# A selective-scan block on one core: pairs of states added by accumulating DMAs instead of by GpSimd

## The chip, the cores and the metric

The kernel runs on one core of a Trainium2 chip. A core has five engines that each work through their own queue in order: TensorE (PE, with its weight loads as PEld), VectorE (DVE), ScalarE (ACT), GpSimd (POOL) and SyncE (SP, which here only issues DMAs). Sixteen DMA engines move data. The metric is the device time of one execution in microseconds. Three runs of the kernel before gave 1902.2 us (median), 1901.79 us (lowest) and 1904.03 us (highest).

## The reference

The input x is (128, 64, 256): 128 sequences of 64 steps and 256 channels, all in float32. Two blocks follow each other, both steered by one condition vector of 512 numbers per sequence.

The first is a linear attention with 16 heads: layer norm, three projections, a softmax of q over the 16 channels of a head and of k over the 64 steps (masked), two small products for each head, a layer norm scaled and shifted by the condition, a projection, and x added back.

The second is a Mamba layer. After a modulated layer norm and a permutation of the steps it computes, cut to what matters here:

```python
xm, z = split(h @ W_in, 2)                 # 512 channels each
xm = silu(conv4(xm) + conv_b)
dtr, Bm, Cm = split(xm @ W_xp, [64, 80])   # 64, 16 and 16 columns
dt = softplus(dtr @ W_dt + b_dt)
A = -exp(A_log)                            # 512 channels x 16 states
# for every step t:
hst = hst * exp(dt_t * A) + (dt_t * x_t) * B_t     # 512 x 16 states
y_t = sum over the 16 states of hst * C_t
y = (y + xm * D_param) * silu(z)
out = x + gate * unpermute(y @ W_out)
```

The recurrence has 128 x 512 x 16 independent states of 64 steps each. They are multiplied by C and added up over the 16 states of a channel. The change touches that sum.

## The kernel before

**Groups.** The 128 sequences are worked in 16 groups of 8 (`NG`, `NB`). For each group, `prepare` computes everything up to dt, w = dt * x, B and C. `scan` does the recurrence, once for each half of the group (4 sequences), and `finish` does the output projection, the gate and the store.

**The scan.** In one half, the loop `m` runs over four blocks of 128 channels and the loop `x` over the two 64-channel halves of a block. One pair (m, x) has one tile `hs` of 128 partitions x (2 x 2 x 8 x 64): partition = 64 channels x 2 halves of the states, then `ii` (two pairs of sequences), sequence in the pair, 8 states (`SJ`), 64 steps. A tile holds 2048 numbers per partition, 1 MB in all. For each `ii`:

- TensorE multiplies `uT` by `diag` and so writes the input term into `hb`, two banks of PSUM (two such buffers);
- ScalarE has made `decay`, the exponentials, 8 instructions for each tile;
- VectorE runs one `tensor_tensor_scan` of 128 x 1024;
- the product with C (`ct`) is made either by VectorE, out of PSUM, or by GpSimd ("apart"), in place in `hs`. The set `APART` gives GpSimd 12 of the 16 products of a half, so 24 of the 32 of a group.

When both `ii` are done and (half, m) is in `PAIRED` (all but half 1, m = 3), GpSimd adds the upper four of the eight states of the tile to the lower four, 128 x 1024 again. TensorE then adds what is left, and the two halves of the states, into `yacc`: with `fold` as weights it runs over j = 0..3 (over 8 states where no pairs were added) for both x. VectorE multiplies `yacc` by silu(z).

There are four `hs` buffers (`NHS`), three `decay` buffers, three `dt2` and four `ct` buffers, two `hb` and one `yacc`.

**Order.** Nothing is left to a scheduler at run time. The class `Plan` records every call as a node; units such as the eight matmuls of one `hb` are one node. The table `ORDER` gives each node of each part (`scan0`, `prepare` and so on) a place, `PERIOD` (100000) being one group, and `order()` lists the nodes by place, holding back those whose inputs or buffers are not there yet. Each engine's queue is that list cut to its own instructions, so `prepare` of later groups is interleaved with the scans. All recorded instructions carry the line of `emit()` in the profile (L486), so groups of instructions are told apart by the names of their tiles.

All loads and stores are issued by SP: `dt2` and `ct` of the scans come back out of HBM (`dt_d`, `c_d`) with each partition half or broadcast that the scan needs.

Of the kernel before, what the change touches and what calls it, by code (L numbers as in the profile page):

```python
# [12 lines left out]
ALU = mybir.AluOpType  # L13
# [4 lines left out]
B, T, D, E = 128, 64, 256, 512  # L18
# [7 lines left out]
NG = B // NB  # L26
KD = D // P
KE = E // P
KI = DI // P
HD = P // 2  # L30
NC = DI // HD
SJ = DS // 2
# [4 lines left out]
APART = {(m, x, 1 - x) for m in range(KI) for x in range(2)} | {(m, 0, 0) for m in range(4)}  # L37
PAIRED = {(h, m) for h in range(2) for m in range(KI)} - {(1, 3)}
# [13 lines left out]
        -995092, -990106, -990248, -972121, -595796, -212864, -174753, -196191, -212939,  # L52
        -961099, -963028, -647496, -239082, -809048, -585679, -903380, -392982, -995853,
        -998690, -998658, -978564, -998761, -1000000, -972303, -1000000, -971839, -998153,
        -992335, -995851, -808931, -992190, -997171, -819048, -989678, -634347, -998162,
        -993953, -989802, -449288, -1000000, -1000000, -789091, -987936, -370078, -825915,
        -678524, -613218, -698586, -662425, -968759, -606956, -473579, -999671, -999858,
        -990255, -998888, -1000000, -1000000, -994652, -999181, -1000000, -985837, -960273,
        -998934, -999181, -977310, -993627, -944637, -971780, -811427, -664040, -784771,
        -664039, -677889, -888439, -689643, -663391, -840908, -663146, -663413, -727553,  # L60
        -663328, -789092, -832193, -851274, -740157, -1000000, -964818, -974366, -731822,
        -991350, -862414, -944797, -1000000, -921394, -812212, -380935, -379583, -183624,
        -176975,
    ],
    "first0": [
        -1000000, -978376, -630660, -998627, -997704, -1000000, -1000000, -1000000, -997299,
        -996885, -999569, -990645, -1000000, -996822, -999447, -994659, -989968, -998495,
        -987832, -959171, -958623, -976292, -981641, -975857, -960993, -985546, -959733,
        -995015, -963408, -949376, -970868, -999959, -953582, -955776, -993088, -953651,
        -944012, -970225, -1000000, -944938, -979597, -934713, -951862, -947285, -943580,  # L70
        -940278, -995331, -833149, -933011, -946878, -857180, -908964, -902556, -965635,
        -819890, -819889, -819891, -737922, -740147, -744759, -714085, -731823, -763169,
        -872482, -767462, -755421, -755080, -770282, -776097, -653828, -571415, -712761,
        -732409, -727706, -749172, -755428, -731824, -729395, -672745, -471240, -405022,
        -408492, -488949, -405021, -370547, -645082, 46765, -640238, -723310, -763006, -782420,
        -754953, -774218, -760167, -340878, -371799, -759582, -766127, -751948, -776216,
        -776050, -776898, -754988, -340856, -341375, -290888, -210442, -361958, -210446,
        -188783, -211959, -188951, -177248, -213375, -188950, -192852, -204116, -196189,
        -187951, -211128, -204115, -208765, -208765, -188958, -178898, -163476, -180505,
        -158338, -165498, -145454, -155745, -145454, -172674, -146435, -126094, -127959,  # L80
        -172671, -145457, -155746, -133032, -154259, -138626, -127958, -133490, -232875,
        -133033, -144477, -156111, -773778, -126843, -123327, -132724, -119680, -1000000,
        -118311, -118822, -133033, -140386, -895462, -117437, -118344, -133405, -95145, -991619,
        -92484, -93161,
    ],
    "first2": [
        -989917, -914702, -325416, -961231, -898579, -969532, -956870, -935784, -960145,
        -999952, -793395, -785227, -1000000, -993454, -946566, -953153, -948506, -938449,
        -939387, -758886, -792923, -687377, -766280, -667266, -630921, -638864, -565697,
        -769280, -446058, -462407, -440447, -811646, -624057, -561269, -488663, -432081,  # L90
        -435680, -401509, -796577, -486505, -426280, -431834, -395880, -434914, -490816,
        -399758, -353104, -240433, -380946, -417054, -360040, -431462, -367222, -397314,
        -358066, -357955, -211127, -358065, -351132, -343370, -274423, -208764, -335285,
        -346455, -775180, -772723, -765469, -764949, -778615, -198584, -203309, -774446,
        -782667, -983648, -984891, -982282, -984450, -980988, -165217, -178508, -123412,
        -147465, -178443, -145453, -155852, -127265, -57778, -132562, -158314, -978503, -988197,
        -978277, -997227, -998661, -119700, -118821, -993949, -980523, -117713, -113567,
        -126885, -114336, -117349, -107072, -107049, -104840, -101480, -116857, -101599, -90423,
        -89609, -86117, -79331, -79567, -121935, -96516, -95027, -94510, -94006, -93342, -92924,
        -105967, -92054, -85660, -137236, -96517, -95039, -94637, -94094, -57435, -73060,  # L100
        -51702, -90005, -50756, -49688, -69739, -69740, -88328, -48446, -45829, -630507, -26868,
        -18979, -46514, -53088, -42764, -50412, -205762, -989257, 6466, -35323, -44427, -216090,
        -984626, 8399, -25010, -42762, -95308, -984980, 8489, 16549, -42761, -74750, -672321,
        9524, -14450,
    ],
    "scan0_first": [
        -128446, -162321, -151313, -139747, -132474, -182139, -144153, -163187, -122764,
        -120446, -122763, -122741, -122775, -122619, -122759, -122742, -133003, -112983,
        -156884, -165753, -108962, -112179, -115646, -119159, -119978, -113196, -116946,
        -111650, -116947, -107108, -111854, -255984, -109585, -110801, -163615, -117229,  # L110
        -103941, -105375, -101837, -96833, -111020, -92232, -277702, -233357, -106504, -111651,
        -107071, -106505, -107097, -104186, -107048, -104879, -252777, -123872, -108466,
        -122522, -99858, -192554, -441320, -101598, -98871, -96846, -106013, -98873, -101829,
        -102382, -101479, -153484, -99862, -186581, -105117, -107253, -93200, -116016, -80008,
        -80006, -53963, -35228, -99131, -109970, -91775, -80007, -93795, -93376, -101175,
        -88674, -96847, -96832, -89984, -46602, -134677, -62212, -44885, -43484, -190998,
        -96509, -94571, -93795, -88329, -96510, -96769, -94573, -94572, -40567, -39885, -30010,
        -94992, -45773, -140866, -20555, -85810, -1094, 10253, -38273, -131760, -128140, -93313,
        -90382, -93377, -93269, -74516, -88328, -88673, -89608, -39386, -74983, -42626, -43686,
        -81144, -27441, 9922, -25352, -27196, -39947, -27596, -39184, -22373, -26684, -30454,  # L120
        8401, 9790, -1426, -36436, -19644, 10273, -4455, 11186, -34099, 19364, -24524,
    ],
    "finish0_first": [
        135714, 27333, 126520, 135825, 160280, 161813, 21135, 495636,
    ],
    "scan1_first": [
        -411767, -317259, -15340, -452280, -353099, -25361, -473315, -347887, -48840, -89188,
        -13745, -59991, -27083, -29839, 6232, -59649, 10975, -75102, 19200, 11087, -821,
        -297741, -291099, 1780, -13121, -25608, -18694, 7747, -13412, 131, -12218, 10789, 4646,
        -309099, 11434, -160608, -105030, -152161, 24753, 8163, 33100, -44420, -264583, -215312,  # L130
        13333, 11181, 12647, 13277, -35685, 11118, -12268, 13544, 21792, -121531, -114359,
        18780, -101067, -155325, -57931, -21737, -5479, 14694, 26131, 11762, -22060, -24964,
        14539, 23071, -106218, 33427, 32746, -80584, -142524, 22028, 43491, -129616, 49509,
        -18791, -272321, -261752, 15526, 3471, 31319, -25503, 20208, 30558, 27720, 29985, 42577,
        -35042, -143989, 36726, -30002, -135919, -582334, 40363, 40602, 30962, 37930, 39676,
        43084, 47815, 32963, 50445, 59070, 48398, 41875, 61090, 36526, -377950, 54088, 65664,
        73884, 105441, -235375, -166644, 43077, 44885, 13734, 44774, 45454, 48182, 47616, 40078,
# [1171 lines left out]
```

## Time and profile before

| what | before |
|---|---|
| three runs, median (lowest to highest) | 1902.2 us (1901.79 to 1904.03) |
| the profiled execution: span from its first to its last instruction | 1900.2 us |
| busy, share of the span: PE | 1768.6 us, 93% |
| DVE | 1770.5 us, 93% |
| ACT | 1703.3 us, 90% |
| POOL | 1769.5 us, 93% |
| DMA: share of the 16 engines on SP's queue | 25.6% |
| products on POOL (hs <- hs,ct) | 384 of 2367 ns |
| pair additions on POOL (hs <- hs) | 224 of 2363 ns |
| products on DVE (hs <- hb,ct) | 128 of 1223 ns |
| scans on DVE | 512 of 2273 to 2275 ns |

The median of the three runs is 2.0 us above the span of the profiled execution. "Busy" is the time in which at least one instruction of the engine runs; instructions that only issue a DMA, wait or load a register are not counted. "Idle before" a group is the time for which the engine stood still just ahead of its instructions, and the releaser is what ended that wait. A wait line reads: engine and tile that waited, whom it waited for, microseconds in all, how many times, the longest.

### The profile page before, as it was taken

Reading aid. Unit: us, or ns where it says so; the run is one execution under the profiler, and the core shown is the slowest. Engines: PE = TensorE matmul, PEld = TensorE weight load, DVE = VectorE, ACT = ScalarE, POOL = GpSimd, SP = SyncE. Lnnn points to the kernel's source line nnn. Section 1 sums busy time; section 2 is a strip of 40 time slices with the busy share of each in tenths; the row PEclk is TensorE's granted clock in tenths of the full one; section 3 lists DMA queues with packets and bytes.
Section 4 is the critical chain, followed back from the end, with each engine's and each line's share of the span. In section 5 each row is a group of like instructions: output and inputs, shape, how many; then the busy total and the mean of one; then the engine's idle time right before and its main releaser. Section 6 shows DMA issues by size and latency. Waiting matters only on the chain.

```text
span 1900.2 us, 32360 instructions
## 1 busy us (share of the span) xinstructions
PE 1768.6 (93%) x11304; PEld 927.5 (49%) x11304; DVE 1770.5 (93%) x1625; ACT 1703.3 (90%) x3996; POOL 1769.5 (93%) x1440
## 2 busy tenths in 40 slices
PE   7788999999999999999999999999999999999776
PEld 5454544545454454545545454554545445454333
DVE  6579899999999999999999999999999999999886
ACT  5889999998999999899999989999899999989762
POOL 3579899999999999999999999999999999999996
PEclk9899999999999999999999999999999999999998
DMA  5311322204132230323213132220413222041320
GB/s 148 80 51 40 79 82 71 79 21 126 42 88 74 63 95 26 109 61 87 74 43 98 37 101 68 82 79 26 115 38 87 82 74 78 20 119 37 102 63 12
DMA packets 173291, 135.71 MB, mean 71 GB/s; under 512 B 30820, under 2 KB 157272, under 8 KB 173128
## 3 DMA queue, kind: packets, MB, share of 16 engines
q1 hardware_dynamic: 173128, 133.64, 25.6%
q8 instruction: 90, 1.47, 0.3%
q14 instruction: 73, 0.60, 0.1%
HBM read 98.84 MB, written 34.75 MB: 70 GB/s over the span
## 4 chain that ended last, share of the span: by engine, by line
POOL 38%; ACT 28%; PE 10%; DVE 8%; issue 6%; DMA 3%; SPq 0%; POOLq 0%; DVEq 0%; ACTq 0%
POOL hs L486 28%; ACT decay L486 13%; DVE hs L486 4%; POOL diag L486 3%; ACT h L486 3%; POOL w L486 3%; DVE xz L486 3%; PE hb L486 2%; ACT kT L486 2%; ACT L482 2%; DVE hb L486 2%; ACT xz L486 2%; PE zp L486 2%; PE kp L486 1%; ACT xn L486 1%
## 5 line engine op out<-in xcount | busy, mean ns | idle before, releaser
L486 ACT ACTIVATE decay<-dt,nA 128x252 f32<-128x252 f32 x2048 | 865.9, 501 | 60.7 <-DMA dt<-dt_d 38.9
L486 POOL TENSOR_TENSOR hs<-hs,ct 128x1024 f32<-128x1024 f32 x384 | 900.7, 2367 | 14.8 <-DVE hs L486 14.7
L486 DVE TENSOR_TENSOR_SCAN hs<-decay,hb 128x1024 f32<-128x1024 f32 x384 | 863.0, 2273 | 38.6 <-PE hb L486 24.6
L486 PE MATMUL hb<-diag,uT 64*64 64x512 f32 x4096 | 532.2, 614 | 68.0 <-DVE hs L486 67.1
L486 POOL TENSOR_TENSOR hs<-hs 128x1024 f32<-128x1024 f32 x224 | 525.8, 2363 | 6.1 <-DVE hs L486 1.1
L486 PE MATMUL yacc<-hs,fold 128*64 128x256 f32 x2304 | 284.6, 392 | 17.2 <-ACT yacc L486 13.9
L486 DVE TENSOR_TENSOR_SCAN hb<-decay,hb 128x1024 f32<-128x1024 f32 x128 | 291.1, 2275 | 4.6 <-PE hb L486 4.6
L486 PEld LDWEIGHTS hb<-diag,uT 64*64 64x64 f32 x4096 | 120.6, 132 | 332.1 <-DVE hs L486 148.3
L486 PEld LDWEIGHTS yacc<-hs,fold 128*64 128x64 f32 x2304 | 163.8, 139 | 147.3 <-POOL hs L486 56.2
L482 ACT ACT_TABLE_LOAD x158 | 202.7, 1283 | 3.4 <-PEq L1297 0.8
L486 DVE TENSOR_TENSOR hs<-hb,ct 128x1024 f32<-128x1024 f32 x128 | 156.5, 1223 | 7.9 <-PE yacc L486 3.2
L486 DVE SCALAR_TENSOR_TENSOR xz<-xp,vec,xz 128x504 f32<-128x504 f32 (+5 forms) x204 | 140.2, 698 | 9.5 <-ACT xz L486 5.2
L486 POOL TENSOR_TENSOR diag<-fold,bT 128x1024 f32<-128x1024 f32 x64 | 121.3, 1909 | 12.9 <-ACT bT L486 12.9
L486 PE MATMUL zp<-h,win 128*128 128x512 f32 (+1 forms) x272 | 120.1, 575 | 1.1 <-DVE xz L486 1.1
L486 PE MATMUL xp<-h,win 128*128 128x512 f32 (+1 forms) x272 | 119.2, 580 | 0.7 <-DVE xz L486 0.6
L486 PE MATMUL yop<-wout,xz 128*128 128x256 f32 x512 | 117.5, 383 | 0.0
L486 PEld LDWEIGHTS yop<-wout,xz 128*128 128x128 f32 x512 | 94.7, 190 | 25.2 <-ACT decay L486 10.6
L486 POOL TENSOR_TENSOR w<-dt,xz 128x512 f32<-128x512 f32 (+1 forms) x68 | 82.0, 1217 | 14.3 <-ACT dt L486 11.2
L486 ACT ACTIVATE yacc<-xz,vec 128x256 f32<-128x256 f32 x128 | 61.0, 477 | 33.1 <-PE yacc L486 33.0
L486 ACT ACTIVATE h<-gtp,mods 128x64 f32<-128x64 f32 x256 | 78.8, 418 | 3.9 <-PE gtp L486 3.9
L486 PEld LDWEIGHTS zp<-h,win 128*128 128x128 f32 x272 | 49.7, 190 | 65.9 <-issue 62.6
L486 PEld LDWEIGHTS xp<-h,win 128*128 128x128 f32 x272 | 48.7, 189 | 67.3 <-issue 47.6
(145 smaller groups left out, 2358.7 us busy)
## 6 DMA issues: line engine op xcount, KB each, us to landing
ct<-c_d SPq DMA_DIRECT2D x128, 256.0 KB
dt<-dt_d SPq DMA_DIRECT2D x256, 128.0 KB
dt_d<-dt SPq DMA_DIRECT2D x60, 256.0 KB
ga<-gate_d SPq DMA_DIRECT2D x64, 128.0 KB
xr<-x_d SPq DMA_DIRECT2D x32, 256.0 KB
out<-xr SPq DMA_DIRECT2D x32, 256.0 KB
xt<-in_x SPq DMA_DIRECT2D x15, 512.0 KB
x_d<-xt SPq DMA_DIRECT2D x15, 512.0 KB
```

The lines of the kernel that those rows point to most:

```text
L482: engine.preload_act_table_set(loaded)
L486: getattr(engine, method)(*real, **kreal)
```

## The change

The pair addition is no longer an instruction on GpSimd's vector path. GpSimd issues a DMA that reads the upper four states of the tile and adds them to the lower four in SBUF. In each tile it moves 128 partitions x 4 runs of 256 numbers, 512 runs of 1 KB. It is issued for the same (half, m) as before, so 224 times. The products are divided anew: VectorE keeps 5 of the 32 of a group (`ON_VECTOR`), GpSimd makes 27. The last group has sets of its own, which hold the same members. The table `ORDER` is replaced throughout. Buffers, matmuls, scans, exponentials and SP's DMAs are the same in number and shape.

```diff
-APART = {(m, x, 1 - x) for m in range(KI) for x in range(2)} | {(m, 0, 0) for m in range(4)}
-PAIRED = {(h, m) for h in range(2) for m in range(KI)} - {(1, 3)}
+ALONE = {(1, 3)}
+ON_VECTOR = {(0, 0, 1, 1), (0, 2, 1, 1), (1, 0, 1, 1), (1, 1, 1, 1), (1, 3, 1, 1)}
+ALONE_LAST = {(1, 3)}
+ON_VECTOR_LAST = {(0, 0, 1, 1), (0, 2, 1, 1), (1, 0, 1, 1), (1, 1, 1, 1), (1, 3, 1, 1)}
...
 ORDER = {
     "setup": [
...
     def scan(g, half):
+        alone, on_vector = (
+            (ALONE_LAST, ON_VECTOR_LAST) if g == NG - 1 else (ALONE, ON_VECTOR)
+        )
...
-                    apart = (m, x, ii) in APART
+                    apart = (half, m, x, ii) not in on_vector
...
                 ready = pl.writers(hs[:, 0])
-                if (half, m) in PAIRED:
-                    pl.gpsimd.tensor_tensor(
-                        hs[:, :, :, : SJ // 2, :].rearrange("p i b j t -> p (i b) (j t)"),
-                        hs[:, :, :, : SJ // 2, :].rearrange("p i b j t -> p (i b) (j t)"),
-                        hs[:, :, :, SJ // 2 :, :].rearrange("p i b j t -> p (i b) (j t)"),
-                        op=ALU.add,
-                    )
+                if (half, m) not in alone:
+                    pairs = hs.rearrange("p i b j t -> p (i b) (j t)")
+                    near, far = pairs[:, :, : SJ // 2 * T], pairs[:, :, SJ // 2 * T :]
+                    pl.gpsimd.dma_start(out=near, in_=far, accum_op=ALU.add)
...
-            last = SJ // 2 if (half, m) in PAIRED else SJ
+            last = SJ if (half, m) in alone else SJ // 2
```

The numbers of `ORDER` are left out here. Where the text speaks of the new order, it means the list that they give on each engine.

## The prediction

> **What bounds the kernel now.** I read first the table of windows, because a share over the whole span mixes stages. Columns: window, its length, then the busy us of PE, PEld, DVE, ACT and POOL (number of instructions), the granted clock, the DMA share and GB/s.
>
> ```profile
> 200.00:1700.00 1500.00, 1443.07 (x9378) 756.54 (x9375) 1456.94 (x1299) 1414.00 (x3317) 1460.84 (x1145) 1.00 0.27 73
> 1700.00:1800.00 100.00, 86.16 (x534) 38.83 (x530) 91.31 (x68) 88.73 (x197) 97.50 (x61) 0.98 0.25 74
> 1800.00:1900.00 100.00, 73.34 (x456) 35.21 (x450) 77.53 (x51) 43.65 (x108) 83.04 (x37) 0.89 0.13 39
> ```
>
> From 200 to 1700 us four engines are all but full: POOL 97.4%, DVE 97.1%, PE 96.2%, ACT 94.3%. Only in the last 200 us does one stand out: POOL, with 180.5 us of work against 168.8 on DVE. Second, the groups by line and shape (busy us, mean ns of one | idle before):
>
> ```profile
> L486 POOL TENSOR_TENSOR hs<-hs,ct 128x1024 f32<-128x1024 f32 x384 | 900.7, 2367 | 14.8 <-DVE hs L486 14.7
> L486 POOL TENSOR_TENSOR hs<-hs 128x1024 f32<-128x1024 f32 x224 | 525.8, 2363 | 6.1 <-DVE hs L486 1.1
> L486 DVE TENSOR_TENSOR hs<-hb,ct 128x1024 f32<-128x1024 f32 x128 | 156.5, 1223 | 7.9 <-PE yacc L486 3.2
> ```
>
> Products and pair additions are 1426.5 us of POOL, 89.2 us for each of 16 groups. The same instructions fill 1174.6 us of the window from 200 to 1700 (windows of the tile hs alone), so it holds 1174.6 / 89.2 = 13.2 groups and one group lasts 113.6 us. In each group POOL works 110.7 us, DVE 110.4, PE 109.3, ACT 107.1. Taking work off POOL alone can therefore win at most 113.6 - 109.3 = 4.3 us of a group: PE is next. Third, the waits:
>
> ```profile
> PEld hb L486 <- DVE hs L486: 148.3, 121, 4.0
> PE hb L486 <- DVE hs L486: 67.1, 83, 3.8
> PEld yacc L486 <- POOL hs L486: 56.2, 53, 3.0
> ACT decay L486 <- DMA dt<-dt_d: 38.9, 34, 4.2
> ```
>
> PE stands still mostly for DVE to free hb, and its weight loads wait 56.2 us for the pair additions: PE reaches yacc while POOL is still adding. Fourth, SP's queue, for what a DMA costs (start, us, instruction):
>
> ```profile
> 985.88 0.34 SPq L486 DMA_DIRECT2D c_d<-xd  x1
> 987.60 1.26 SPq L486 DMA_DIRECT2D ct<-c_d  x2
> 990.71 0.34 SPq L486 DMA_DIRECT2D dt_d<-dt  x1
> 993.45 1.22 SPq L486 DMA_DIRECT2D dt<-dt_d  x2
> L486 SPq DMA_DIRECT2D ct<-c_d x128: 573/592/1464, 67.1 to 1817.6; - x128
> ```
>
> A load that needs a store is issued once the store has landed: 1.72 us after its issue for the 32 KB of c_d, 2.74 us for the 256 KB of dt_d. The last line is min/median/max of an issue: 592 ns for ct, a transfer of 64 x 8 = 512 runs.
>
> **The change, part by part.**
>
> 1. Pair additions leave POOL's vector path: 14 a group x 2.363 = 33.1 us off POOL.
>
> 2. Three more products a group move from DVE to POOL: 3 x 2.367 = 7.1 us onto POOL, 3 x 1.223 = 3.7 us off DVE. DVE falls to 106.7.
>
> 3. In place of each addition POOL issues a DMA of 512 runs. No row shows POOL issuing one, so call its price x. Below it is bounded by SP's 0.59 us for as many runs, above by 2.36 us, POOL's whole pass over the same half tiles; a price over that isn't excluded, because the reads name both source and destination, and a negative one is, because the queue is in order. I take 1.2 us: the row nearest in kind is SP's issue, and POOL needs twice as long as another engine for the same thing in the rows we have (2.367 against 1.223 for a product). POOL then has 110.7 - 33.1 + 7.1 + 14x = 84.7 + 14x = 101.5 us a group. It stays the bound only from x = (110.7 - 84.7) / 14 = 1.86 us. The Trainium skill ("DMA: Bandwidth & Descriptors", Specifications) puts the first byte of GpSimd's path at about 1 us against 0.6 on SP's; as an estimate from that page x would be 1.0 and POOL 98.7 us.
>
> 4. The sum arrives later. The addition took 2.36 us. The two landing times above (stores to HBM, the nearest rows) give 1.72 + (2.74 - 1.72) x 480/224 = 3.9 us for 512 KB, SP's 0.34 us of issue in it. Reading the destination as well as the source can double the moved part (2.3 us more): 3.9 to 6.2, of which I take the middle, 5.0, and with POOL's slower issue (1.2 - 0.34) it is 5.9 us, 3.5 more than the addition. The Trainium skill speaks against this step: "Collectives: The Full Stack", Part 3, says that a reduce by DMA runs at half a copy's rate because it reads two sources; by that page alone I would stand at the upper end, 7.1 us with the issue. No run here shows it yet.
>
> Who waits for that: PE at yacc, with the hb matmuls of later tiles queued behind it, and behind those DVE, which has two hb (4.5 us of scans) in hand. From the last hb matmul of an m to its yacc, PE must be busy for a scan (2.27), a product (2.37 on POOL, 1.22 on DVE) and the sum. Before, that is 7.0 us, or 5.9 where DVE makes the product. The old order has about 6 us of PE work there in the shortest two places (half 0 m = 3, half 1 m = 1) and 10 or more elsewhere, counted with the matmul rows (8 matmuls of hb 1.09 us, 16 of yacc 1.95). The new order has about 7 at (1,1), 11.5 at (1,0), 12 at (0,3), 13 to 20 elsewhere. The new chain is 10.5 us, or 9.4 at (1,1) and (1,0), whose last product is DVE's: PE loses 9.4 - 7.1 = 2.3 us a group at (1,1) and nothing elsewhere.
>
> 5. The four hs buffers. One tile every 7.1 us gives each 28.4 us. It needs 4.5 (scans) + 2.4 + 5.9 + 7.1 (the other x) + 2 (yacc) = 21.9 us, so in the steady part this is covered by 6.5 us. In the last group, without prepare, a tile comes every 5.3 us (85 us of DVE work in 16 tiles): 21.2 us against 20.1. There the cover is gone.
>
> 6. DMA traffic: 224 x 0.5 MB is 117 MB moved once more, 117/134 of the present 25.6% if read once (22 points), 45 points if both are read: 48 to 71% of the 16 engines. They are not full, but dt2 arrives later behind such bursts; ACT's 38.9 us could double. ACT has 6.5 us of slack a group, so I cost 2.4 us more of its waits a group at nothing. Should ACT be the bound, it would cost that much, 34 us.
>
> Everything else keeps its count (158 table loads, all matmuls, all of SP's DMAs), so it costs nothing as long as the new places are no worse; a micro-stall of 1 us a group is in the sum for them.
>
> **Sum.** Steady part: PE 109.3 + 2.3 + 1.0 = 112.6 us a group against 113.6; over 14 groups -14 us. The last 200 us hold 163.6 / 89.2 = 1.83 groups: POOL's 180.5 us fall by 1.83 x (26.0 - 16.8) = 16.8 to 163.7, DVE's to 162. The tight buffers of step 5 and the later sums eat most of that; I take -6 us. Span 1900.2 - 20 = 1880; with the 2.0 us by which the median of the runs stands above it, 1882 us. At its best (PE at the 98.4% that POOL reached in its fullest 100 us, no wait at yacc) a group lasts 111.1: -35, tail -12, 1855. At its worst within this case (ACT's waits partly showing, no gain in the tail) 1898.
>
> **Rivals.**
>
> A. As forecast: POOL is freed, PE becomes the bound. For it: 26 us a group leave POOL's vector path. Against: only 4.3 us can be won. 1855 to 1898. Chance 0.50.
>
> B. The issue is the new bound, on POOL's queue. Nothing in the trace prices it; it decides from x = 1.86. At x = 2.1 POOL has 114.1 us, at its 97.4% 117.1 a group: +3.5 x 14 = +49, 1951. At 2.4, 118.3/0.974 = 121.5: +7.9 x 14 = +110, 2012. Against: SP's 0.59 for as many runs. Just above 1.86 it is 1906. Chance 0.22.
>
> C. The landing is longer than 5 us and PE stands before yacc. It decides from a loss of 3.3 us a group, a chain of 10.4 at (1,1), that is a sum (issue and landing) of 6.9 us. At 9 us the three short places lose 5.4 + 1.0 + 1.6 = 8.0: 109.3 + 8.0 + 1.0 = 118.3, +4.7 x 14 = +66, 1968. For it: both operands are read, and slices of the DMA row stand at 7 to 9 tenths. Against: the new order already leaves 12 us at (0,3), where the old left 6. 1906 to 1968. Chance 0.22.
>
> D. Gain and waits cancel: within 0.2%, 1898.4 to 1906.0. Chance 0.06.
>
> **How the numbers follow.** 0.2% (3.8 us) is about what a measurement of this kernel can tell from no change. Faster 0.50 (A), same 0.06 (D), slower 0.44 (B and C). The forecast is A's, 1882 us, its own range 1855 to 1898. The range for 8 in 10 starts there and reaches through most of B and C to 1985, leaving out B from x = 2.26 on and a little of A below 1855.
>
> **What would show it.** Right: POOL's busy time near 1769.5 - 525.8 + 113.6 = 1357 us with 432 products of 2.37 us; 224 DMAs on POOL's queue whose issue holds it for 1.2 us or so; PE at 97 to 98% between 200 and 1700, its waits before yacc named by a DMA and under 3 us a group; a group of 112.6 us. B: POOL's queue without idle time though its busy share is 71%, DVE and PE waiting for products. C: yacc <- DMA in the waits with well over 100 us, POOL idle, hb and then DVE late. The forecast is wrong if DVE or ACT, not PE, is the fullest engine of the steady part.

## The result, and the profile after

The changed kernel takes 1968.6 us (median; 1962.6 to 1969.0), the kernel before, run beside it, 1902.3 us. The ratio is 1.034, 95% interval 1.0326 to 1.0355. The forecast was 1882 us and faster. The time lies inside the range, 1855 to 1985, but on the slower side: at the upper end of rival C.

Windows of the changed kernel, with the columns of the table of before (length, busy us of PE, PEld, DVE, ACT, POOL, clock, DMA share, GB/s):

```profile
200.00:1700.00 1500.00, 1420.34 (x9029) 738.42 (x9026) 1368.41 (x1217) 1373.58 (x3202) 1333.36 (x1160) 0.99 0.71 133
1700.00:1800.00 100.00, 92.63 (x617) 49.72 (x617) 89.80 (x79) 87.72 (x220) 89.34 (x71) 1.00 0.73 136
1800.00:1900.00 100.00, 78.77 (x480) 34.85 (x476) 79.18 (x52) 69.50 (x151) 84.76 (x45) 0.91 0.70 129
```

No engine is full any more: PE 94.7%, ACT 91.6%, DVE 91.2%, POOL 88.9%. All four have lost busy share together. One group, counted from its first xz on VectorE to the next group's (mean from group 3 to 14), lasts 116.25 us; by the same count it lasted 112.24 before (the prediction read 113.6). That is 4.0 us for each of some 13 groups, 52 us. Another 4 us are lost ahead of group 1, and the stretch from the last group's first xz to the end has grown from 90.4 to 98.1 us.

The groups that were costed (busy us, mean ns of one | idle time before):

```profile
L485 POOL TENSOR_TENSOR hs<-hs,ct 128x1024 f32<-128x1024 f32 x432 | 1055.4, 2499 | 85.0 <-DVE hs L485 77.0 <-issue 7.7
L485 POOL DMA_DIRECT2D hs<-hs x224 | 292.0, 1400 | 71.7 <-DVE hs L485 29.7 <-POOL hs L485 26.0 <-DVE xz L485 9.6
L485 DVE TENSOR_TENSOR hs<-hb,ct 128x1024 f32<-128x1024 f32 x80 | 97.5, 1218 | 9.7 <-PE yacc L485 6.1 <-PE htp L485 2.6 <-POOL hs L485 0.2
```

The additions are gone, 432 products stand on POOL and 80 on DVE, as planned. Of the tile hs on POOL the instructions themselves (min/median/max ns) and the landings, then the DMA queues (packets, MB, share of 16 engines):

```profile
L485 POOL DMA_DIRECT2D hs<-hs x224: 1242/1297/1829, 93.4 to 1949.4; - x112
DMA to landing us min/median/max: 5.4/6.0/12.5
```

```profile
q0 software_dynamic: 118272, 117.45, 41.6%
q1 hardware_dynamic: 173128, 133.64, 26.0%
```

An issue takes 1.30 us (median; the mean, in the groups above, is 1.40) and its sum is there 6.0 us after the start of the issue (median). The waits (us in all, times, longest), with line two as it was before at the end:

```profile
POOL hs L485 <- DVE hs L485: 106.7, 97, 3.5
DVE xz L485 <- PE yacc L485: 76.4, 23, 6.6
ACT decay L485 <- DMA dt<-dt_d: 39.5, 20, 4.6
PE yacc L485 <- DMA hs<-hs: 38.7, 20, 3.8
...
DVE xz L486 <- PE yacc L486: 10.3, 5, 3.5
```

Line two is the one that has grown most on VectorE. POOL, which stood still for 39 us between 200 and 1700 us before (1500 - 1460.84), now does so for 167 us there, much of it waiting for VectorE (line one). The timeline of one group shows how line two arises (start, length, engine, instruction, idle time before it and who ended it):

```profile
1065.02 7.00 POOL L485 TENSOR_TENSOR hs<-hs,ct 128x1024 f32<-128x1024 f32 x3 [0.25 <-DVE hs L485]
1072.06 0.20 POOL L485 TENSOR_TENSOR dm<-st 128x4 f32<-128x4 f32 x1
...
1074.55 0.20 POOL L485 TENSOR_TENSOR rt<-r 128x4 f32<-128x4 f32 x1 [0.68 <-ACT r L485]
...
1075.66 0.20 POOL L485 TENSOR_TENSOR mu<-mu,rt 128x4 f32<-128x4 f32 x1
1075.80 2.63 POOL L485 DMA_DIRECT2D hs<-hs  x2
...
1085.10 2.59 PE L485 MATMUL yacc<-hs,fold 128*64 128x256 f32 x16 [2.14 <-DMA hs<-hs]
...
1087.73 0.42 DVE L485 TENSOR_TENSOR xz<-yacc,xz 128x256 f32<-128x256 f32 x1 [3.72 <-PE yacc L485]
```

The same place before:

```profile
925.79 7.00 POOL L486 TENSOR_TENSOR hs<-hs,ct 128x1024 f32<-128x1024 f32 x3
...
937.44 4.68 POOL L486 TENSOR_TENSOR hs<-hs 128x1024 f32<-128x1024 f32 x2
...
942.46 1.95 PE L486 MATMUL yacc<-hs,fold 128*64 128x256 f32 x16
...
945.63 0.41 DVE L486 TENSOR_TENSOR xz<-yacc,xz 128x256 f32<-128x256 f32 x1
```

The longer timeline is half 0, m = 2, written (0,2) below. The products end at 1072.02. Then POOL's queue holds fourteen small instructions of the normalising chain of the next groups (dm, ve, mu, rt), which wait for ScalarE's r in their midst. Only then, 3.8 us behind the products, are both DMAs issued, the second 0.84 us after the first. The second is the one of x = 0; its own last product ended 7.0 us before it (the 7.1 us of some expectations below), but the last product of x = 1 stands between. PE stands still 2.14 us for them, and VectorE, whose queue has xz in front, 3.72 us. Taken from the instructions of groups 2 to 14, the mean times at (0,2) are:

| | last product to last issue | issue to landing | landing to yacc | VectorE idle before xz |
|---|---|---|---|---|
| before (addition) | 6.9 | 2.4 | 0.3 | 0 |
| after | 4.8 | 8.7 | 0.1 | 4.16 |

Before and after, the issue stands behind a chain of small instructions. What has grown is the time from the last product to the sum: 9.2 us before, 13.5 after. At the six other places VectorE's idle time before xz is 0.18 us or less.

The wait has a second price. The 16 matmuls of yacc, 1.95 us before, take 2.59 us in the timeline above. A window of 4 us from their midst on (columns as in the table of windows; 0.57 is the granted clock):

```profile
1086.00:1090.00 4.00, 4.00 (x22) 1.61 (x19) 2.27 (x2) 2.32 (x6) 4.00 (x4) 0.57 0.51 183
```

From 200 to 1700 us the granted clock is 0.5 for 30.7 us in eight stretches, seven of them 3.4 us long, and every one begins around a yacc at (0,2) that PE had waited for. In the kernel before there is no such stretch in this window. In the eight groups concerned these matmuls take 3.27 us and VectorE stands still 4.8 us; in the five others from 2 to 14 it is 2.04 and 3.1 us. No run separates this from the length of the wait.

### The profile page after: what moved, and what is told of

Its sections match the earlier page's. It is cut to its first block, busy times and chain, and to the rows that moved or that the text cites. A ratio compares the mean times of both kernels' runs of the same rounds, so it can differ in the third digit from the quotient of the medians.

```text
span 1966.8 us, 32617 instructions
## 1 busy us (share of the span) xinstructions
PE 1800.6 (92%) x11304; PEld 940.8 (48%) x11304; DVE 1715.7 (87%) x1577; ACT 1706.6 (87%) x3996; POOL 1661.0 (84%) x1488
## 3 DMA queue, kind: packets, MB, share of 16 engines
q0 software_dynamic: 118272, 117.45, 41.6%
q1 hardware_dynamic: 173128, 133.64, 26.0%
## 5 line engine op out<-in xcount | busy, mean ns | idle before, releaser
L485 POOL TENSOR_TENSOR hs<-hs,ct 128x1024 f32<-128x1024 f32 x432 | 1055.4, 2499 | 85.0 <-DVE hs L485 77.0
L485 DVE TENSOR_TENSOR_SCAN hs<-decay,hb 128x1024 f32<-128x1024 f32 x432 | 971.0, 2274 | 80.2 <-ACT decay L485 26.8
L485 ACT ACTIVATE decay<-dt,nA 128x252 f32<-128x252 f32 x2048 | 868.5, 504 | 61.3 <-DMA dt<-dt_d 39.5
L485 PE MATMUL hb<-diag,uT 64*64 64x512 f32 x4096 | 546.6, 621 | 73.9 <-DVE hs L485 71.3
L485 POOL DMA_DIRECT2D hs<-hs x224 | 292.0, 1400 | 71.7 <-DVE hs L485 29.7
L485 PE MATMUL yacc<-hs,fold 128*64 128x256 f32 x2304 | 307.2, 402 | 47.7 <-DMA hs<-hs 38.7
L485 PEld LDWEIGHTS yacc<-hs,fold 128*64 128x64 f32 x2304 | 185.0, 142 | 178.6 <-issue 87.8
L485 DVE TENSOR_TENSOR_SCAN hb<-decay,hb 128x1024 f32<-128x1024 f32 x80 | 182.3, 2278 | 4.6 <-ACT decay L485 1.9
L485 DVE SCALAR_TENSOR_TENSOR xz<-xp,vec,xz 128x488 f32<-128x488 f32 (+5 forms) x204 | 137.7, 696 | 6.9 <-ACT xz L485 4.6
L485 DVE TENSOR_TENSOR xz<-yacc,xz 128x256 f32<-128x256 f32 x128 | 52.9, 413 | 77.4 <-PE yacc L485 76.4
L485 DVE TENSOR_TENSOR hs<-hb,ct 128x1024 f32<-128x1024 f32 x80 | 97.5, 1218 | 9.7 <-PE yacc L485 6.1
L485 ACT ACTIVATE yacc<-xz,vec 128x256 f32<-128x256 f32 x128 | 59.7, 466 | 45.5 <-PE yacc L485 45.5
```

The source lines that it names most:

```text
L485: getattr(engine, method)(*real, **kreal)
```

## The experiments

Theory: the sums are late at (0,2), and what they cost there is most of the loss. Rivals: the issues on POOL; the DMA traffic; the new order itself; PE as the bound. Ratios are to the kernel before, run beside each; a difference "in us" is the ratio applied to 1902.2.

**Sums that nobody waits for.** The DMA adds the lower half onto the upper half, which is not read again; half of the states are left out of the sum.

```diff
-pl.gpsimd.dma_start(out=near, in_=far, accum_op=ALU.add)
+pl.gpsimd.dma_start(out=far, in_=near, accum_op=ALU.add)
```

> The changed kernel, but each accumulating DMA adds the lower four states to the upper four, which nobody reads afterwards. So half of the states are left out of the sum; issue, size and traffic of the 224 DMAs stay, and TensorE no longer waits for any of them (the tile is still freed only when its DMA has read it). Late sums (they reach TensorE 3 to 6 us later than the additions did): the 4.2 us a group that VectorE stands before xz at half 0, m = 2 and TensorE's 38.7 us of waits for DMAs go, 1885 to 1915 us. Issue or traffic (GpSimd's queue or loads slowed down by 117 MB more): nothing changes, 1960 to 1970 us. New places bad in themselves: 1950 us or more.

Measured: 1908.3 us, ratio 1.0029 (1.0014 to 1.0044), 112.4 us a group. Same issues, same bytes, same order: waiting for the sums costs 3.1%, 59 us (the clock included: here it has no stretch at 0.5 between 200 and 1700 us). But with all those waits gone the kernel is still no faster than before, so the waits are not the only step that failed.

**No sums at all.** The DMA is not issued; half of the states are left out.

```diff
 for method, args, kw in n.calls:
+    if "accum_op" in kw:
+        continue
```

> The changed kernel with neither DMA nor addition: half of the states are left out of yacc (output without them), the order, the 27 products and everything else are those of the changed kernel. It tells what the DMAs themselves cost when nobody waits for their sums (1908 us with them). Theory 'issue and traffic': 14 issues of about 1.3 us a group and 117 MB more are what holds that kernel at 112.4 us a group; without them a group lasts 108 to 110.5 us and the kernel 1850 to 1880 us. Rival 'the new order is no faster': DVE stands still for other reasons (decay, hb, the turn behind yacc), a group stays at 111.5 to 112.5 us and the kernel takes 1890 to 1910 us.

Measured: 1872.8 us, ratio 0.985 (0.9836 to 0.9865), 110.4 us a group. Window:

```profile
200.00:1700.00 1500.00, 1468.03 (x9521) 757.24 (x9520) 1433.76 (x1278) 1433.91 (x3375) 1152.45 (x1025) 1.00 0.27 73
```

Here PE is at 97.9% and POOL at 76.8%. Relieved of all 33 us of sums a group, the new order gains 1.8 us a group. The DMAs cost 34 us even when nobody waits for them (0.985 to 1.0029).

**A quarter of the bytes**, and **a GpSimd pass of the same length**, both on the run with unread sums.

```diff
-pl.gpsimd.dma_start(out=far, in_=near, accum_op=ALU.add)
+pl.gpsimd.dma_start(out=far[:, :, :T], in_=near[:, :, :T], accum_op=ALU.add)   # quarter
+n = SJ // 2 * T * 11 // 16                                                     # pass
+pl.gpsimd.tensor_tensor(far[:, :, :n], far[:, :, :n], near[:, :, :n], op=ALU.add)
```

> The kernel with unread sums (1908 us; 1873 us with no DMAs at all), with each DMA moving a quarter of the bytes: the first 64 of each 256 numbers, the same 512 runs. Half of the states are left out of yacc, as there. Those 35 us are either GpSimd's time for 14 issues a group or the traffic, behind which dt2 arrives late. Theory 'traffic': ScalarE's waits for dt2 fall from 35 us to under 15, 1880 to 1895 us. Rival 'issue': 1900 to 1910 us.

> The counterpart: the kernel with unread sums, each DMA replaced by a GpSimd addition of 11/16 of the half tile into the states that nobody reads, about 1.63 us, as long as the issue and the gap ahead of it (1.30 + 0.30). No DMA traffic is added; half of the states are left out of yacc. Theory 'traffic': 1873 to 1885 us, ScalarE's waits for dt2 under 10 us. Rival 'issue': GpSimd's queue is what costs, 1895 to 1910 us.

Measured: quarter 1883.1 us, ratio 0.9884 (0.9861 to 0.9906); pass 1905.4 us, ratio 1.0005 (0.999 to 1.0019). The issue takes 1.30 us with a quarter of the bytes as well, so 28 of the 34 us go with the bytes (each of these differences is good to about 5 us). Waits of the run with unread sums, then of the one with a quarter of the bytes:

```profile
ACT decay L485 <- DMA dt<-dt_d: 35.1, 17, 5.7
DVE hs L485 <- ACT decay L485: 26.9, 17, 3.2
```

```profile
DVE hs L485 <- ACT decay L485: 12.2, 9, 2.8
...
ACT decay L485 <- DMA dt<-dt_d: 8.8, 5, 3.6
```

The loads of dt2 come late behind the bursts, the exponentials with them, and VectorE's scans with those. Without any sums the first of these waits is 5.6 us. VectorE's part of this chain falls by 14.7 us, half of the 28, and the end of the kernel by about 8 us: it takes 93.4 us with all the bytes and 85.2 with a quarter. For a tile that an accumulating DMA still holds VectorE waits 4.1 us in all in the run with all the bytes, so that is not where they cost. The pass speaks against "traffic alone": a pass of 1.69 us, without a byte of traffic, costs 30 us. That POOL's time is free in this order is refuted. But the two holds are not equal. The ends of two products with a pass between them are 4.09 us apart, with an issue 3.99. Where two follow each other, as at (0,1) and (0,2), two passes hold the queue for 3.32 us and two issues for 2.63; at 49 such pairs that makes 34 us. In the pass run ScalarE waits 22.6 us for ve and 11.5 for mu, in the quarter run 5.7 for ve. So the pass does not price an issue; the quarter run bounds it, with 6.5 us for all issues and a quarter of the bytes. How the 23 us between the two runs are made up was not tested.

**The place (0,2).** Four runs. First, both issues right behind their products, ahead of the normalising chain:

```diff
+for i in (94, 109):
+    ORDER["scan0"][i] = -40000
```

> The changed kernel with two entries of ORDER changed: in half 0, m = 2 of groups 1 to 14 the two DMAs are issued right behind the products they wait for, not 7.1 us later behind the two chains of small normalising instructions on GpSimd. Late sums: the landing comes 5 to 6 us earlier, VectorE's 4.2 us of wait a group before xz shrink to 0 to 1, so about 45 to 55 us less, 1910 to 1925 us; if other places are nearly as tight, 1925 to 1945. New places bad in themselves, or issue and traffic: 1960 to 1970 us, since all of that stays.

Measured: 1952.4 us, ratio 1.0262 (1.0237 to 1.0286): a miss. VectorE's gap before xz falls from 4.2 to 0.95 us a group, but the wait moves on:

```profile
DVE hs L487 <- ACT decay L487: 54.8, 34, 3.2
...
ACT r L487 <- POOL ve L487: 32.6, 21, 3.0
```

ScalarE now waits for ve, which stands behind two issues, and its exponentials come later (26.8 us of VectorE's waits before the move). Second, additions by POOL at (0,2) and DMAs elsewhere:

```diff
+if (half, m) != (0, 2):
     pl.gpsimd.dma_start(out=near, in_=far, accum_op=ALU.add)
+else:
+    pl.gpsimd.tensor_tensor(near, near, far, op=ALU.add)
```

> The changed kernel, but at half 0, m = 2 GpSimd adds the pairs itself, in the same place of its queue; the other six (half, m) keep their DMAs. The sum is then there 2.4 us after GpSimd starts it instead of 8.7 us. Late sums at this one place: VectorE's 4.2 us a group before xz go, nothing is issued ahead of the normalising chain (unlike the early issue), so 1908 to 1925 us. GpSimd's queue is what matters (two additions hold it 4.7 us, two issues 2.6): 1945 to 1970 us, since the additions hold the queue longer.

Measured: 1949.4 us, ratio 1.0237 (1.022 to 1.0254): a miss again. The sum is in time, 3.6 us ahead of yacc, and still the gap before xz is 2.04 us. The two passes now hold up the chain behind them: ScalarE waits 27.2 us for mu, and PE's transposes of what ScalarE then makes (xtp <- xn) stand ahead of yacc. Third and fourth, the two issues apart. The one of x = 0 goes between the products; the one of x = 1 goes behind ve ("split"), or stays where it is ("first only").

```diff
+ORDER["scan0"][94] = 61000
+ORDER["scan0"][109] = 63180     # split only
```

> The changed kernel with the two DMAs of half 0, m = 2 apart: the one of x = 0 issued right behind its own two products, ahead of the last product of x = 1, the one of x = 1 behind the part of the normalising chain that ScalarE waits for (ve), ahead of rt. Theory 'late sums at one place': the gap of VectorE before xz there falls from 4.2 us a group to under 1, and unlike with both issues ahead of the chain ScalarE's r is not late; a group of 112.5 to 114 us, 1905 to 1935 us. Rival 'the wait only moves': the first issue delays the last product and r as before, 1945 to 1960 us.

> The changed kernel with one of the two DMAs of half 0, m = 2 moved: that of x = 0 is issued right behind its own two products; that of x = 1 stays behind the normalising chain. Both moved, with the second ahead of rt, gave 1933 us and new waits of ScalarE for mu and ve (19 us). Theory 'the price at this place is two landings together and the order in GpSimd's queue': the second DMA is now alone and lands 5.5 to 6 us after its issue instead of 8.7, so VectorE's gap before xz falls from 4.2 to 1 to 2 us a group while ScalarE's new waits are halved; 1915 to 1940 us. Rival 'the 7 us behind the chain alone decide': the gap stays above 3 us, 1950 to 1965 us.

Measured: split 1933.1 us, ratio 1.0177 (1.0151 to 1.0203); first only 1926.0 us, ratio 1.0105 (1.0081 to 1.013). Waits of the second:

```profile
DVE xz L486 <- PE yacc L486: 31.4, 23, 5.3
...
PE yacc L486 <- DMA hs<-hs: 10.3, 9, 2.4
```

| at (0,2) | last product to last issue | issue to landing | landing to yacc | idle before xz |
|---|---|---|---|---|
| unread sums | 5.1 | 8.6 | -2.4 (not waited for) | 0.86 |
| split | 1.1 | 5.6 | 4.1 | 0.86 |
| first only | 3.0 | 5.9 | 0.9 | 0.86 |

One number of ORDER takes 45 us off (1.034 to 1.0105). The gap falls to the 0.86 us that it has when nobody waits for a sum: 3.3 us x 13 groups = 43 us; the granted clock is 0.5 for 3.4 us of the window from 200 to 1700 us instead of 30.7. Alone, the second DMA lands in 5.9 us instead of 8.7, and the chain, no longer waiting for ScalarE as long, is over sooner. The landing is then 0.9 us ahead of its use, and bringing it still earlier (split) only delays ScalarE.

**Old and new order with the other way of adding.** The additions in the changed kernel's places with 24 products on POOL, and the DMAs in the places of before with 24 products.

```diff
# additions, new places
-pl.gpsimd.dma_start(out=near, in_=far, accum_op=ALU.add)
+pl.gpsimd.tensor_tensor(near, near, far, op=ALU.add)
# DMAs, old places
-pl.gpsimd.tensor_tensor(near, near, far, op=ALU.add)
+pl.gpsimd.dma_start(out=near, in_=far, accum_op=ALU.add)
```

> The places of the changed kernel with the work of the kernel before: GpSimd adds the pairs itself and makes 24 of the 32 products. Late sums: without DMA latency the wait before xz shrinks, but GpSimd has 110.7 us of work a group again, so 1900 to 1925 us. New places bad in themselves: 1945 us or more. Issue or traffic: about 1902 us.

> The kernel before with its places and its 24 products on GpSimd, only the additions replaced by the accumulating DMAs. In the old places the additions of half 0 m = 2 and 3 and of half 1 m = 1 are done 0.3 to 0.6 us before TensorE reads them; a DMA lands 3.5 to 5 us later than they did. Late sums: three tight places a group instead of one, 1975 to 2030 us, slower than the changed kernel. New places bad in themselves: faster than the changed kernel, 1890 to 1940 us. Issue or traffic alone: about 1965 us.

Measured: 2219.3 us, ratio 1.1662 (1.1633 to 1.1691), and 2122.3 us, ratio 1.1152 (1.1118 to 1.1186). With the DMAs in the old places PE waits 162.7 us for them, so late sums do decide there, at a higher price than expected. Additions in the new places say nothing about the DMAs: at (0,3) the last product ends 27 us after its scan. That product is VectorE's in this mix, but its place in the list was made for POOL's queue; POOL stands still for it (18.7 us up to 1114.53, for one), and one of the two hb is held as long. In both runs the granted clock falls as well, to 0.94 and 0.96 on average from 200 to 1700 us. An order belongs to the instructions that it was listed for; crossing the two tells little of either.

**Is PE the bound?** The output projection yop over half of its channels (58.8 us less for PE; the other half is left out), in the kernel before and in the run with unread sums.

```diff
-for k in range(KI):
+for k in range(KI // 2):
```

> The kernel before with the output projection (yop) over half of its channels only: half of that product is left out, 58.8 us less work on TensorE, 3.7 us a group. If TensorE sets the pace of the group before: 1845 to 1865 us. If GpSimd and VectorE, at 97% of the steady part, set it: 1885 to 1900 us.

> The same cut of the output projection in the variant of the changed kernel whose DMAs write where nobody reads (half of the states and half of the projection are left out). There GpSimd is freed and nobody waits for a sum, and still it took 1908 us. If TensorE took over as the bound: 1850 to 1870 us. If the coupling of the queues (small waits everywhere, no full engine) sets the pace: 1890 us or more.

Measured: 1905.8 us, ratio 1.0004 (0.9993 to 1.0016), and 1915.7 us, ratio 1.0056 (1.0034 to 1.0079). 3.7 us less for PE in each group give nothing. The granted clock is 0.5 for 27 and 44 us of the window in these two runs and never in the runs they are set against, which takes part of the relief back; but the groups without such a stretch last 112.4 and 112.2 us, against 112.24 and 112.4, so they gain next to nothing either. Then the reverse, on "first only": TensorE adds all eight states itself at (1,1), or at (1,1) and (1,0), and no DMAs are issued there.

```diff
+if (half, m) in ON_TENSOR:      # {(1, 1)} or {(1, 0), (1, 1)}
+    last = step = SJ
```

> The kernel with the first DMA at half 0, m = 2 moved (1926 us), and at half 1, m = 1, where the sums land 0.1 us before their use, no DMAs: TensorE adds all eight states there, 1.95 us more a group, and xz has 6.7 us in hand behind it. Two issues and a seventh of the traffic go. Theory 'traffic and issues cost 35 us in all and TensorE is not the bound': 4 to 15 us less, 1910 to 1922 us. Rival 'TensorE is full': 1.95 us a group show up, 1930 to 1955 us.

> As the run before, and at half 1, m = 0 too (8.5 us in hand for xz there): TensorE works 3.9 us more a group, GpSimd issues 10 DMAs instead of 14. Theory 'traffic and issues': 1898 to 1918 us, the best version of the new order with sums. Rival 'TensorE is full' (96.5% in the run with the first DMA moved, so 113.3 - 109.3 = 4 us a group at most are free): 1930 to 1980 us.

Measured: 1937.5 us, ratio 1.0173 (1.0155 to 1.0192), and 1968.5 us, ratio 1.0329 (1.0312 to 1.0346). 16 x 1.95 = 31 us more of yacc cost 13 us at the first place and 30 us more at the second, although two issues and a seventh of the traffic went each time. With both, in all and at (1,0) in one group:

```profile
DVE hs L487 <- PE yacc L487: 67.1, 44, 3.4
...
1113.79 1.95 PE L487 MATMUL hb<-diag,uT 64*64 64x512 f32 x16
1115.66 3.67 PE L487 MATMUL yacc<-hs,fold 128*64 128x256 f32 x32
...
1119.47 2.29 DVE L487 TENSOR_TENSOR_SCAN hs<-decay,hb 128x1024 f32<-128x1024 f32 x1 [2.24 <-PE yacc L487]
```

The first line was 20.0 us in "first only". The scan has its hb (made by 1115.74) and starts when yacc ends: what it needs of yacc is the hs tile that yacc reads, one of the four, to write into. At (1,1) it is a product on VectorE that waits in the same way. So it is not PE's total that counts but where the work stands: work taken from yop wins nothing, and work put into yacc keeps hs buffers that VectorE is waiting for.

**Freeing POOL in the old order.** DMAs at (0,0) and (1,0) only, where the addition was 7.6 and 4.7 us ahead of its use.

```diff
+if (half, m) in {(0, 0), (1, 0)}:
+    pl.gpsimd.dma_start(out=near, in_=far, accum_op=ALU.add)
+else:
     pl.gpsimd.tensor_tensor(near, near, far, op=ALU.add)
```

> The kernel before, its places and its 24 products, with DMAs only at half 0 m = 0 and half 1 m = 0, where the additions were done 7.6 and 4.7 us before TensorE read them; a DMA lands 3.6 us later. Late sums as the whole cost: no place waits, GpSimd is relieved of 3 us a group, 1893 to 1902 us, the best so far. If an issue costs the queue more than it shows (products behind it slowed, traffic): 1905 us or more.

Measured: 1910.1 us, ratio 1.0031 (1.0019 to 1.0042), the second of the two expectations.

```profile
200.00:1700.00 1500.00, 1443.13 (x9384) 758.58 (x9384) 1456.62 (x1299) 1416.07 (x3318) 1409.51 (x1150) 1.00 0.41 91
```

POOL's busy time falls by 51 us, VectorE's 1457 and the group (112.15 us) stay, 4 us are lost ahead of group 1. VectorE is the fullest, so it was relieved next: the same DMAs, in groups 2 to 13 only, and one or two more products on POOL.

```diff
-apart = (m, x, ii) in APART
+apart = (m, x, ii) in APART or ((half, m, x, ii) in MOVED and 2 <= g <= 13)
# MOVED: {(0, 0, 1, 1)}, or {(0, 0, 1, 1), (0, 1, 1, 1)}
```

> The kernel before, its own order, with DMAs in place of additions only at m = 0 of both halves and only in groups 2 to 13, and there one product more (half 0, m = 0, x = 1, second pair) on GpSimd instead of VectorE: VectorE loses 1.22 us a group, GpSimd gains 2.37 and loses about 4 x (2.36 - 1.6) = 3. Theory 'VectorE bounds the kernel before' (it was busy 97.1% and freeing GpSimd or TensorE alone changed nothing): a group lasts 111.0 to 111.4 us instead of 112.2, so 1885 to 1897 us. Rival 'several engines hold each other': freeing one engine by 1.2 us gives nothing, 1900 to 1910 us.

> As the run with one product moved, and a second product (half 0, m = 1, x = 1, second pair) on GpSimd too in groups 2 to 13: VectorE loses 2.45 us a group, GpSimd gains 4.7 and loses 3, so it stands where it stood before plus 1.7 us. Theory 'VectorE bounds': 110.3 to 111.5 us a group, 1875 to 1895 us, if GpSimd is not late at m = 2. Rival 'GpSimd is late at m = 2, where the sum came 0.3 us before its use': the second product gives its gain back or more, 1900 to 1925 us.

Measured: 1910.8 us, ratio 1.0051 (1.0036 to 1.0066), and 1945.5 us, ratio 1.0234 (1.0217 to 1.0251). VectorE has 1.2 us less in each group, and a group lasts 0.9 us longer: it waits 18 us for another matmul (bd <- ap; 2.8 before). With two products, which is slower than either expectation, ScalarE waits 60 us for ve between 200 and 1700 us (23 before) and VectorE 45.5 us for yacc (2.3 before), and the granted clock is 0.5 for 72 us of that window. Neither PE, POOL nor VectorE can be relieved alone in the old order.

**The ends.** On "first only", no DMAs in the first and last group; TensorE adds all eight states.

```diff
+if g in (0, NG - 1):
+    last = step = SJ
```

> The run with only the first DMA moved, and in the first and the last group no DMAs: TensorE adds all eight states there (1.95 us more for each of 7 places, with TensorE at 73% in the last 100 us). After the last group's first xz the changed kernel needs 98.1 us against 90.4 before. Theory: the end costs 86 to 92 us and the whole kernel 4 to 12 us less than the run with the first DMA moved. Rival: the extra matmuls stand ahead of other work and nothing is gained, within 3 us of that run.

Measured: 1940.7 us, ratio 1.019 (1.0165 to 1.0215), a miss: the end takes 103.1 us instead of 96.3 and group 1 starts 5 us later.

No version that computes every state beats the kernel before.

## Why the prediction was wrong, step by step

What the runs put in place of the sum, in us of 1902.2 (differences of the ratios; by their 95% intervals the first row is good to 3 us, the others to 5 or 6):

| from | to | us |
|---|---|---|
| before | new order, no sums | -28.5 |
| no sums | issues and a quarter of the bytes, unread | +6.5 |
| quarter | all bytes, unread | +27.6 |
| unread | waited for, (0,2) mended ("first only") | +14.5 |
| (0,2) mended | the changed kernel | +44.7 |
| sum (of the rows before rounding) | | +64.7 |

What makes up the 14.5 us no run takes apart.

- **Steps 1 and 2** (33.1 us off POOL, three products moved) held: 432 and 80 products at 2.37 and 1.22 us in the median. The mean of the 432 is 2.50, because a product right behind an issue takes 2.87.
- **Step 3** (issue x = 1.2 us) held: 1.30 us, or 1.67 by its effect on the next product; both are under the 1.86 from which POOL would be the bound. POOL works 1333.36/1500 x 116.25 = 103.3 us a group (101.5 forecast). Rival B is out. The estimate of 1.0 from the Trainium skill ("DMA: Bandwidth & Descriptors", Specifications) was a little low.
- **Step 4, the landing** (5.9 us with the issue) held for a DMA by itself: 5.9 us in the median of 128. But 96 of the 224 have another within 3 us, and those take 7.8 (8.7 at (0,2)). The 7.1 us worked out from the Trainium skill ("Collectives: The Full Stack", Part 3, half a copy's rate) lies between the two. The trace agrees with the rule better in the engines' own time: 41.6% of 16 engines' 1966.8 us for 117.45 MB is 1.8 times the time per byte that SP's queue takes (26.0% for 133.64 MB), whose packets are of other sizes.
- **Step 4, who waits, is the step that failed**: "PE loses 9.4 - 7.1 = 2.3 us a group at (1,1) and nothing elsewhere". At (1,1) the sum is there 0.1 us before its use and VectorE loses nothing, with 6.8 us in hand at xz there. At (0,2), costed at nothing, VectorE stands still 4.2 us a group, 3.3 more than without sums. The count there set PE's work between hb and yacc (13 to 20 us) against scan + product + sum (10.5). Two terms of that chain were wrong. The place of the issue in POOL's queue was put at nothing: it starts 4.8 us behind the last product, behind small instructions that wait for ScalarE and behind the other issue. And the landing was that of one DMA, 5.9 us, where two go out together and the second takes 8.7. With both the chain is 18.1 us. The queue's part could be seen in the trace of before (6.9 us), with a 2.4 us addition behind it and 0.3 us to spare. The step also looked for the loss on PE (38.7 us) where VectorE, in order, stood still for twice that (76.4, of which 22.0 without any sums too), and it had no term for the lower clock behind such a wait.
- **Step 5** (hs buffers): the "cover" of 6.5 us in the steady part is not there at (1,0) and (1,1). VectorE's waits for yacc ahead of scans and products, most of them at these two places, are 18.1 us without any sums and 20.2 in the changed kernel, 4.5 before; the runs with TensorE adding there show what more of it costs. In the last group no run takes it alone. The end, forecast to gain 6 us, lost 8; with a quarter of the bytes and unread sums it takes 85.2 us, so bytes and waits are what cost there.
- **Step 6** (DMA share 48 to 71%) held in size, 71% from 200 to 1700 us (67.6% of the whole span), and failed in price: costed at nothing, the bytes take 28 us. The wait to look at was not "ACT's 38.9 us" of the old order, which stayed at 39.5. The new order without sums has only 5.6 us there, and the traffic brings 30 back.
- **Sum**: the group of before was read too long, 113.6 us where counting from xz to xz gives 112.24. With it every number per group is 1.2% too long (PE's 109.3 is 108.0), which all but cancels in the differences. The new order does gain with POOL relieved, 1.8 us a group of the 4.3 that the profile allowed. "PE becomes the bound" was too simple: 3.7 us less of it gave nothing, 1.95 more in yacc cost.
- **Rival C** had the right mechanism and nearly the time (1968), from a landing of 9 us at "three short places". It was one place, and its sign in the profile was VectorE's wait for yacc, not a PE wait "well over 100 us".

## What to carry to other kernels

When a computation becomes a DMA, follow the queue of the engine that issues it: count what stands between the last producer and the issue, and whether another DMA goes out at the same moment, before counting what the consumer has in hand. Then look for the loss on the last in-order engine of the chain rather than on the one that reads the data, and at the granted clock behind the wait. Where four engines are at 94 to 97%, work taken from one of them is worth nothing until the runs show which queue place it frees, and DMA traffic that "fits" still delays the small loads that share the engines.

## What the runs showed of the hardware

- An accumulating DMA of 512 runs holds GpSimd 1.30 us, whether a run is 1 KB or 256 bytes (both medians 1.30). Behind a product GpSimd also stands still 0.30 us before it. The next instruction starts about 0.8 us into the issue but takes 0.5 us longer (a product 2.87 instead of 2.37 us). The ends of two products with an issue between them are 3.99 us apart, without one 2.32: 1.67 us more. Two issues that follow each other start 0.85 us apart and take 2.63 us together (49 pairs).
- The landing, counted from the start of the issue: 512 KB alone 5.9 us, 128 KB 3.6 us; with a second one within 3 us, 7.8 and 4.1 us.
- In the engines' shares a packet of the 1 KB runs costs 0.416 x 1966.8 x 16 / 118272 = 0.111 us and one of the 256 byte runs 0.200 x 1880.5 x 16 / 118272 = 0.051 us: a quarter of the bytes is still nearly half of the time.
- In the changed kernel the granted TensorE clock fell to 0.5 for 3.4 us (once 6.8) around yacc at (0,2) in eight of the groups 2 to 14, where PE had stood still 2.1 to 3.8 us for a DMA; waits of the same length went without it in the five others (1.5 to 3.3 us).
